# A decoder block on one core: the attention's projections, the fold of V and the output projection as four column tiles of 32

## Chip, cores and metric

The kernel runs on one NeuronCore of a Trainium2 chip, everything in float32. Times are device microseconds of one execution. For the kernel before, the median of three runs is 2486.4 us (2485.95 to 2489.06).

## What is computed

The reference is a decoder layer with three blocks, each followed by a residual addition and a layer norm. Cut to what matters here:

```python
# x: (4, 1024, 512); 32 heads of 16
q = lin(lin(x, wq_w, wq_b), vq_w, vq_b)     # k and v alike
scores = einsum('cbqh,cbkh->cbqk', q, k) / sqrt(16)
o = einsum('cbqk,cbkh->cbqh', softmax(scores), v)
x = layernorm(x + lin(o, wo_w, wo_b))
x = layernorm(x + gated_convolution(x, ctx))        # two taps, four gates
x = layernorm(x + quantised_feed_forward(x))
```

Only the attention and its projections are touched by the change.

## The kernel before

**Set-up (L297 to L352).** The two linear maps in front of q, k and v are multiplied into one matrix each. For q and k this happens at once (L344, matmuls of the whole array, 512 columns wide). For v it is left to small pieces: `fold_v` (L394) makes 128 rows by 256 columns of the folded matrix `w_v`.

**Units (L357).** The attention works on 32 units: 4 batches by 8 groups of 4 heads. A unit's q and k lie in four quadrants of 32 partitions, one per head (16 rows of the head, a row for the softmax's maximum, and padding). For each unit three things are done on TensorE:

- `nat` (L436): scores with queries on the partitions, whose row maxima VectorE reduces at L465. A head's contraction is 32 rows deep, so each multiplication uses a row tile of the array, 32 rows by 128 columns. One call makes two heads, 512 keys each.
- `scores` (L502): scores with keys on the partitions, again in row tiles, 256 queries wide (L519). ScalarE makes the exponentials from them (L530).
- `weigh` (L535): the exponentials times v. The contraction is over 128 keys and the result is 16 values and a sum per head, so four heads stand side by side: each multiplication uses a column tile of 128 rows by 32 columns and writes 32 partitions of the tile `av` (L545). One call is 16 multiplications: 4 blocks of keys, 4 heads in turn.

**Pieces between them.** Work for later units is cut into pieces of four multiplications that accumulate into one PSUM tile over the 512 features (FT = 4 blocks of 128): `project` (L376, q and k of two units, 176 or 160 tokens wide, evicted by ScalarE at L386), `project_v` (L403, 128 tokens by 256 columns of v, added to its bias by VectorE at L411), `fold_v` (evicted by ScalarE at L401), and `out_piece` (L428), which calls `Handed.project` (L217) for 128 tokens by 256 columns of the output projection. Each of the four multiplications has 128 rows of contraction and a result of 128 partitions, so it uses the whole array. The pieces, `scores` and `weigh` take their PSUM tiles in turn from one pool of four banks, `ps_st` (L354); `nat` has a pool of its own.

**Order.** The attention's order is written out by hand: engines get their instructions as the Python loop emits them. Twelve projection pieces and five folds stand in a row at the start (L619). Then, in units 0 to 30 (L674 to L708), a unit has 32 half-steps. Each half-step emits a `nat` for the next unit and a `scores` for this one. After half-step 1, 5, 9, ... comes a `weigh`, after half-step 3, 7, 11, ... one piece:

```python
for work in (nat(u + 1, i, half), scores(u, i, 1 - half)):
    work()
if h % 4 == 1 and weighing:
    weigh(*weighing.pop(0))
...
if h % 4 == 3:
    weighing.append((u, h // 4))
    if fill:
        fill.pop(0)()
    elif u > 24 or u == 24 and h > 24:
        out_pieces.pop(0)()
```

Unit -1 (before the first) and unit 31 (the last) have loops of 16 steps (L642 to L672). In unit -1 each step has one or two pieces after its `nat` calls. In unit 31 every second step has a `weigh` with an output piece directly behind it.

**After the attention** comes the `tail` (L726): the second half of the output projections (L763, through the same `Handed.project`, 512 columns wide), the gated convolution and the feed-forward block.

How the profile counts: a float32 multiplication of the program is two weight loads (LDWEIGHTS) and two MATMULs in the trace, so a piece has 8 MATMULs and a `weigh` 32.

Of the kernel before, what the change touches and what calls it, by code (L numbers as in the profile page):

```python
# [14 lines left out]
P = 128  # L15
# [3 lines left out]
FT = D // P  # L19
# [9 lines left out]
@with_exitstack  # L29
def decoder_kernel(ctx: ExitStack, tc: tile.TileContext, a, out):  # L30
    nc = tc.nc

    outer = ctx.enter_context(tc.tile_pool(name="outer", bufs=1))
    ident = outer.tile([P, P], F32, tag="ident", name="ident")
    make_identity(nc, ident)
    eps = outer.tile([P, 1], F32, tag="eps", name="eps")
    nc.gpsimd.memset(eps, EPS)

    dram = ctx.enter_context(tc.tile_pool(name="dram", bufs=1, space=bass.MemoryType.DRAM))
    attn_d = [dram.tile([D, S], F32, tag=f"attn{b}", name=f"attn{b}") for b in range(B)]


    shared = ctx.enter_context(tc.tile_pool(name="shared", bufs=1))
    hand = Handed(tc, a, shared, attn_d, eps)
    with ExitStack() as attn:
        attention(attn, tc, a, attn_d, ident, shared, hand)
    with ExitStack() as rest:
        tail(rest, tc, a, out, ident, eps, hand)  # L50


class Handed:
# [160 lines left out]
        nc.vector.tensor_mul(scale, tmp, ok)  # L214
        self.scale, self.inv = scale, inv

    def project(self, b, t, cols, pt, bias=False):  # L217

        nc = self.nc
        attn_t = self.big[b][:, 0 : FT * S].rearrange("p (t s) -> p t s", t=FT)  # L220
        for f in range(FT):
            nc.tensor.matmul(  # L222
                pt, attn_t[:, f, t * P : (t + 1) * P], self.w_o[:, f, cols], start=f == 0, stop=f == FT - 1
            )
        y = self.y[b]
        if bias:
            nc.vector.tensor_add(y[:, t, cols], y[:, t, cols], self.b_o[:, cols])
        nc.vector.tensor_add(y[:, t, cols], pt, y[:, t, cols])
        if cols.stop == D:
            nc.vector.bn_stats(self.stats[b][:, t, :], y[:, t, :])  # L230


def attention(ctx, tc, a, attn_d, ident, shared, hand):
    nc = tc.nc
# [4 lines left out]
    w_v = shared.tile([P, FT, D], F32, tag="w_v", name="w_v")  # L239
# [18 lines left out]
    for i in range(2):  # L258
        t = (once if i else shared).tile([P, NT, NH * VW + 15], F32, tag=f"v_sb{i}", name=f"v_sb{i}")
# [9 lines left out]
    for n, pool in ((3, shared), (1, once)):  # L269
        t = pool.tile([P, 8 if n == 3 else 2, S], F32, tag=f"qk{n}", name=f"qk{n}")  # L270
# [9 lines left out]
    for i in range(2):  # L280
        t = once.tile([P, 32], F32, tag=f"neg{i}", name=f"neg{i}")
        nc.gpsimd.memset(t, 0.0)
        negs.append(t)
    for i in range(2):
        t = once.tile([P, S], F32, tag=f"rbc{i}", name=f"rbc{i}")
# [11 lines left out]
    xts = {}  # L297
# [7 lines left out]
    pt = ps.tile([P, P], F32, tag="ps", name="idle_ps")  # L305
    for n in range(10):
        nc.tensor.matmul(pt, idle, idle, start=True, stop=True)
    for which, (w, v, dst) in enumerate((("wq", "vq", b_q), ("wk", "vk", b_k), ("wv", "vv", None))):
        w_n = sp.tile([P, FT, D], F32, tag="w_n", name=f"w_n{which}")
        v_t = sp.tile([P, FT, D], F32, tag="v_t", name=f"v_t{which}")  # L310
# [48 lines left out]
    QW = 256  # L359
# [4 lines left out]
    def to_quadrants(u, which, packed):  # L364

        dst = (q_ts, k_ts)[which][u % 4]
        for j in range(4):
            h = u % 2 * 4 + j
            nc.sync.dma_start(dst[32 * j : 32 * j + HD, :], packed[h * HD : (h + 1) * HD, :])
        if which == 0 and u >= 4:  # L370
            nc.sync.dma_start(dst[HD::32, :], dst[HD + 1 :: 32, :])
# [4 lines left out]
    def project(p, which, t0, n, packed):  # L376

        b, gg = divmod(p, 4)
        w, bias = ((w_q, b_q), (w_k, b_k))[which]
        cols = slice(t0, t0 + n)  # L380
        pt = ps_st.tile([P, QW], F32, tag="st", name=f"proj{p}_{which}_{t0}")
        for f in range(FT):
            nc.tensor.matmul(  # L383
                pt[:, 0:n], w[:, f, gg * P : (gg + 1) * P], xts[b][:, f, cols], start=f == 0, stop=f == FT - 1
            )
        nc.scalar.activation(packed[:, cols], pt[:, 0:n], AF.Identity, bias=bias[:, gg : gg + 1], scale=1.0)  # L386
        if t0 + n == S:
            to_quadrants(2 * p, which, packed)
            if which == 0 and p > 0:
                late_rows.append(lambda: to_quadrants(2 * p + 1, 0, packed))  # L390
            else:
                to_quadrants(2 * p + 1, which, packed)

    def fold_v(f, half):  # L394
        cols = slice(half * QW, half * QW + QW)
        pt = ps_st.tile([P, QW], F32, tag="st", name=f"fold2_{f}_{half}")
        for m in range(FT):
            nc.tensor.matmul(
                pt, w_n[:, m, f * P : (f + 1) * P], v_t[:, m, cols], start=m == 0, stop=m == FT - 1
            )  # L400
        nc.scalar.copy(w_v[:, f, cols], pt)  # L401

    def project_v(b, t, half):  # L403

        pt = ps_st.tile([P, QW], F32, tag="st", name=f"v{b}_{t}_{half}")
        cols = slice(half * QW, half * QW + QW)
        for f in range(FT):
            nc.tensor.matmul(  # L408
                pt, xts[b][:, f, t * P : (t + 1) * P], w_v[:, f, cols], start=f == 0, stop=f == FT - 1
            )  # L410
        nc.vector.tensor_add(  # L411
            v_sb[b % 2][:, t, 16 * half * VW : 16 * (half + 1) * VW].rearrange("p (c h) -> p c h", h=VW)[
                :, :, 0:HD
            ],
            pt.rearrange("p (c h) -> p c h", h=HD),
            b_v[:, cols].rearrange("p (c h) -> p c h", h=HD),
        )

    def qk_pieces(p, which):


        parts = [(0, 176), (176, 176), (352, 176), (528, 176), (704, 160), (864, 160)]
        return [lambda part=part: project(p, which, *part, packs[:, which, :]) for part in parts]

    def v_pieces(b, t):
        return [lambda half=half: project_v(b, t, half) for half in range(2)]

    def out_piece(b, t, half):  # L428
        pt = ps_st.tile([P, QW], F32, tag="st", name=f"po{b}_{t}_{half}")
        hand.project(b, t, slice(half * QW, half * QW + QW), pt)  # L430

# [180 lines left out]

    outs = [(0, t) for t in range(NT)] + [(2, t) for t in range(NT)]
    out_pieces = [lambda b=b, t=t, half=half: out_piece(b, t, half) for b, t in outs for half in range(2)]

    folds = [lambda f=f, half=half: fold_v(f, half) for f in range(FT) for half in range(2)]
    for piece in qk_pieces(0, 0) + qk_pieces(0, 1) + folds[:5]:  # L619
        piece()  # L620
# [3 lines left out]
    for u in range(-1, NU):  # L624
# [48 lines left out]
        else:  # L673
            for h in range(HS):  # L674
                i, half = divmod(h, 2)
# [343 lines left out]
```

## Time and profile before

| | |
|---|---|
| median of 3 runs | 2486.4 us |
| the profiled execution's own time | 2487.75 us |
| its span, first to last instruction | 2486.0 us |
| mean granted TensorE clock | 0.996 |
| TensorE matmuls, weight loads | 25492 each |
| 126 to 1559 us (attention, units 0 to about 24): busy PE, DVE, ACT | 1429.65, 1023.42, 913.29 us |
| 1559 to 1926 us (rest of the attention up to unit 31): busy PE, DVE, ACT | 364.88, 269.43, 225.64 us |
| 1926 to 1976 us (unit 31): busy PE, DVE, ACT | 48.76, 19.01, 35.51 us |
| 1976 to 2486 us (tail): busy PE, DVE, ACT | 485.41, 367.21, 113.31 us |

PE is TensorE's matmuls, PEld its weight loads, DVE is VectorE, ACT ScalarE, POOL GpSimd and SP SyncE. A row of the groups reads: line, engine, operation, what it writes from what it reads, the shape, how many; then the busy time of the group in us, the mean duration of one in ns, and the idle time of the engine in front of them with what ended it. Shapes of matmuls begin with the part of the array that is used, rows by columns: 32\*128 is a row tile, 128\*32 a column tile, 128\*128 the whole. A row of the timeline reads: start in us, length in us, engine, line, operation and how many were merged into it. The end of a matmul is modelled by the profiler, its start is recorded; so distances between starts are what can be relied on, and "single records" below are starts of single instructions in the trace.

### The profile page before, as it was taken

To read this page: it belongs to the slowest core of one execution; us is meant where nothing else is said; L and a number is where in the kernel's file an instruction comes from. 1 tells how busy PE (TensorE), PEld (TensorE's weight loads), DVE (VectorE), ACT (ScalarE), POOL (GpSimd) and SP (SyncE) were. 2 spreads that over 40 slices of the span, in tenths; PEclk is the share of its full clock that TensorE was granted. 3 is DMA by queue.
4 is the path that set the end of the run, shared out by engine and by line. 5 is a ranking of instruction groups with operands and counts; after the bars stand their busy time and mean duration, and the time that the engine had idled before them with its cause. 6 is when DMAs were issued, how large, how long until landed. Compare 5 with 4: busy or idle time off the path is not lost.

```text
span 2486.0 us, 60152 instructions
## 1 busy us (share of the span) xinstructions
PE 2452.5 (99%) x25492; PEld 1781.1 (72%) x25492; DVE 1748.6 (70%) x2198; ACT 1306.5 (53%) x2558; POOL 333.5 (13%) x275
## 2 busy tenths in 40 slices
PE   9999999999999999999999999999999999999998
PEld 6677777777777777777777776677776799547984
DVE  3767777777777777777777777777777465888568
ACT  1166666666666666666666666666655511411132
POOL 2000000000000000000000002000020265311640
PEclk9999999999999999999999999999999999999999
DMA  6101111111110211101111114110120243240311
GB/s 216 48 11 20 20 25 54 21 23 22 23 26 16 58 21 20 21 20 23 22 21 21 24 20 134 21 24 16 25 79 11 66 157 136 84 153 18 119 35 68
DMA packets 80653, 120.80 MB, mean 49 GB/s; under 512 B 39056, under 2 KB 39056, under 8 KB 80384
## 3 DMA queue, kind: packets, MB, share of 16 engines
q1 hardware_dynamic: 79808, 115.90, 16.5%
q8 instruction: 201, 3.29, 0.6%
q10 hardware_dynamic: 576, 1.05, 0.1%
q14 instruction: 68, 0.56, 0.1%
HBM read 80.77 MB, written 18.35 MB: 40 GB/s over the span
## 4 chain that ended last, share of the span: by engine, by line
PE 91%; DVE 5%; POOL 2%; DMA 0%; ACT 0%; issue 0%; SPq 0%; DVEq 0%; POOLq 0%
PE nat L449 22%; PE av L545 19%; PE st L519 18%; PE proj L383 10%; PE v L408 5%; PE po L222 5%; PE pa L792 5%; PE pc L792 5%; PE fold L344 1%; PE pf L878 1%; POOL w L161 1%; DVE y L116 1%; DVE y L883 1%; DVE y L909 1%; DVE xq L864 1%; DVE stats L884 1%
## 5 line engine op out<-in xcount | busy, mean ns | idle before, releaser
L465 DVE TENSOR_REDUCE mx<-nat 128x2 f32<-128x1024 f32 x1008 | 1187.7, 1219 | 453.2 <-PE st L519 424.4
L530 ACT ACTIVATE at<-st 128x512 f32<-128x512 f32 x2016 | 1042.4, 603 | 625.5 <-PE st L519 610.0
L449 PE MATMUL nat<-qk 32*128 32x512 f32 x4032 | 1013.3, 614 | 3.8 <-DVE mx L465 3.8
L519 PE MATMUL st<-qk 32*128 32x256 f32 x8064 | 999.2, 387 | 0.0
L519 PEld LDWEIGHTS st<-qk 32*128 32x128 f32 x8064 | 656.0, 184 | 45.7 <-issue 3.1
L545 PE MATMUL av<-at,v_sb 128*32 128x256 f32 x8192 | 498.8, 382 | 0.6 <-ACT at L530 0.6
L449 PEld LDWEIGHTS nat<-qk 32*128 32x128 f32 x4032 | 343.3, 184 | 174.1 <-DVE mx L465 120.3
L545 PEld LDWEIGHTS av<-at,v_sb 128*32 128x32 f32 x8192 | 241.3, 110 | 223.4 <-ACT at L530 90.5
L592 POOL TENSOR_TENSOR o_n<-o_sb,rbc 128x512 f32<-128x512 f32 x64 | 96.1, 1523 | 1694.3 <-DMA rbc<-rec_d 1233.9
L383 PE MATMUL proj<-xT,w_qk 128*128 128x176 f32 (+1 forms) x1536 | 270.2, 320 | 0.7 <-ACT w_qk L349 0.7
L383 PEld LDWEIGHTS proj<-xT,w_qk 128*128 128x128 f32 x1536 | 223.7, 189 | 64.6 <-ACT at L530 60.0
L792 PE MATMUL pc<-xf,w 128*128 128x171 f32 x1024 | 161.9, 310 | 6.0 <-DVE u L796 4.4
L792 PE MATMUL pa<-xf,w 128*128 128x171 f32 x1024 | 161.4, 310 | 0.0
L792 PEld LDWEIGHTS pc<-xf,w 128*128 128x128 f32 x1024 | 153.6, 191 | 7.7 <-DVE u L796 4.9
L792 PEld LDWEIGHTS pa<-xf,w 128*128 128x128 f32 x1024 | 153.7, 191 | 0.0
L803 ACT ACTIVATE u<-u,b_c 128x512 f32<-128x512 f32 x64 | 45.5, 720 | 170.7 <-DVE u L802 170.7
L408 PE MATMUL v<-w_v,xT 128*128 128x256 f32 x512 | 126.0, 391 | 0.0
L222 PE MATMUL po<-w_o,big 128*128 128x256 f32 (+1 forms) x384 | 118.9, 459 | 2.1 <-ACT at L530 2.1
L878 PE MATMUL pf<-w_f,xq_t 128*128 128x512 f32 x256 | 117.2, 602 | 3.8 <-DVE y L883 2.3
L408 PEld LDWEIGHTS v<-w_v,xT 128*128 128x128 f32 x512 | 92.5, 189 | 34.4 <-ACT at L530 16.6
L222 PEld LDWEIGHTS po<-w_o,big 128*128 128x128 f32 x384 | 70.3, 190 | 49.2 <-issue 31.6
L558 DVE TENSOR_TENSOR o_sb<-av,o_sb 128x256 f32<-128x256 f32 x128 | 54.3, 424 | 72.0 <-PE av L545 71.5
(97 smaller groups left out, 1213.2 us busy)
## 6 DMA issues: line engine op xcount, KB each, us to landing
qk<-qk SPq DMA_DIRECT2D x256, 64.0 KB
w<-in_conv_wT SPq DMA_DIRECT2D x32, 512.0 KB
u<-in_ctx SPq DMA_DIRECT2D x16, 1024.0 KB
xT<-in_xT SPq DMA_DIRECT2D x16, 512.0 KB
rbc<-rec_d SPq DMA_DIRECT2D x128, 64.0 KB
attn<-o_n SPq DMA_DIRECT2D x256, 32.0 KB
big<-attn SPq DMA_DIRECT2D x4, 2048.0 KB
y<-in_x SPq DMA_DIRECT2D x4, 2048.0 KB
```

The lines of the kernel that those rows point to most:

```text
L222: nc.tensor.matmul(pt, attn_t[:, f, t * P : (t + 1) * P], self.w_o[:, f, cols], start=f == 0, stop=f == FT - 1)
L383: nc.tensor.matmul(pt[:, 0:n], w[:, f, gg * P : (gg + 1) * P], xts[b][:, f, cols], start=f == 0, stop=f == FT - 1)
L408: nc.tensor.matmul(pt, xts[b][:, f, t * P : (t + 1) * P], w_v[:, f, cols], start=f == 0, stop=f == FT - 1)
L449: nc.tensor.matmul(pts[n], q_ts[u % 4][r : r + 32, qt * P : (qt + 1) * P], k_ts[u % 4][r : r + 32, kh * 512 : kh * 512 + 512], start=True, ...
L465: nc.vector.tensor_reduce(mxs[u][:, qt, 2 * pair : 2 * pair + 2, kh], pt, AX.X, ALU.max, negate=True)
L519: nc.tensor.matmul(st[:, k * QW : k * QW + QW], k_ts[u % 4][r : r + 32, kt * P : (kt + 1) * P], q_ts[u % 4][r : r + 32, qq * QW : qq * QW ...
L530: nc.scalar.activation(at, st, AF.Exp, scale=0.25)
L545: nc.tensor.matmul(av[32 * j : 32 * j + 32, :], v_sb[b % 2][:, kt, c * VW : c * VW + 32], ats[u, 2 * i + n // 2, j][:, n % 2 * QW : n % 2 ...
L558: nc.vector.tensor_add(o, av, o)
L592: nc.gpsimd.tensor_mul(o_n[:, :, half * 256 : half * 256 + 256], o_sb[:, cols].rearrange("p (s e) -> p e s", e=2), rbc[:, cols].rearrange( ...
L792: nc.tensor.matmul(pt, w[:, i, tap, o : o + P], xf[:, tap, i, :], start=i == 0, stop=i == FT - 1)
L878: nc.tensor.matmul(pt, xq_ts[b, t][:, f, :], hand.w_f[:, f, :], start=f == 0, stop=f == FT - 1)
```

## The change

A new helper, `by_quarters`, does the four multiplications of a piece as sixteen: for each block of the contraction, four multiplications with 32 columns of the stationary matrix each, that write 32 partitions each of the same PSUM tile. `project`, `fold_v`, `project_v` and `out_piece` use it; the tail's `Handed.project` of 512 columns and the folds of L344 stay as they were. The sums, their order over the features, the moving operands and the evictions are the same.

```diff
+def by_quarters(nc, pt, lhsT, rhs):
+    for f in range(FT):
+        for j in range(4):
+            r = slice(32 * j, 32 * j + 32)
+            nc.tensor.matmul(pt[r, :], lhsT(f)[:, r], rhs(f), start=f == 0, stop=f == FT - 1)
...
-    def project(self, b, t, cols, pt, bias=False):
+    def project(self, b, t, cols, pt, bias=False, quarters=False):
...
-        for f in range(FT):
-            nc.tensor.matmul(
-                pt, attn_t[:, f, t * P : (t + 1) * P], self.w_o[:, f, cols], start=f == 0, stop=f == FT - 1
-            )
+        if quarters:
+            by_quarters(nc, pt, lambda f: attn_t[:, f, t * P : (t + 1) * P], lambda f: self.w_o[:, f, cols])
+        else:
+            for f in range(FT):
+                nc.tensor.matmul(
+                    pt, attn_t[:, f, t * P : (t + 1) * P], self.w_o[:, f, cols], start=f == 0, stop=f == FT - 1
+                )
...
-        for f in range(FT):
-            nc.tensor.matmul(
-                pt[:, 0:n], w[:, f, gg * P : (gg + 1) * P], xts[b][:, f, cols], start=f == 0, stop=f == FT - 1
-            )
+        by_quarters(nc, pt[:, 0:n], lambda f: w[:, f, gg * P : (gg + 1) * P], lambda f: xts[b][:, f, cols])
...
-        for m in range(FT):
-            nc.tensor.matmul(
-                pt, w_n[:, m, f * P : (f + 1) * P], v_t[:, m, cols], start=m == 0, stop=m == FT - 1
-            )
+        by_quarters(nc, pt, lambda m: w_n[:, m, f * P : (f + 1) * P], lambda m: v_t[:, m, cols])
...
-        for f in range(FT):
-            nc.tensor.matmul(
-                pt, xts[b][:, f, t * P : (t + 1) * P], w_v[:, f, cols], start=f == 0, stop=f == FT - 1
-            )
+        by_quarters(nc, pt, lambda f: xts[b][:, f, t * P : (t + 1) * P], lambda f: w_v[:, f, cols])
...
-        hand.project(b, t, slice(half * QW, half * QW + QW), pt)
+        hand.project(b, t, slice(half * QW, half * QW + QW), pt, quarters=True)
```

## The prediction

> **What bounds the kernel now.** I read four views in this order: the page (who is busy, what the chain that ended last is made of), the groups by shape (what one instruction of each kind takes), TensorE's timeline round one piece of each kind, and the durations line by line. The page first:
>
> ```profile
> PE 2452.5 (99%) x25492; PEld 1781.1 (72%) x25492; DVE 1748.6 (70%) x2198; ACT 1306.5 (53%) x2558; POOL 333.5 (13%) x275
> ...
> PE 91%; DVE 5%; POOL 2%; DMA 0%; ACT 0%; issue 0%; SPq 0%; DVEq 0%; POOLq 0%
> PE nat L449 22%; PE av L545 19%; PE st L519 18%; PE proj L383 10%; PE v L408 5%; PE po L222 5%; PE pa L792 5%; PE pc L792 5%; PE fold L344 1%; PE pf L878 1%; POOL w L161 1%; DVE y L116 1%; DVE y L883 1%; DVE y L909 1%; DVE xq L864 1%; DVE stats L884 1%
> ```
>
> TensorE sets the end: 91% of the chain is its own work. Inside the attention it never waits long for anybody; in the list of its waits the score maxima (nat for the reduction of L465) hold it 3.8 us in all. So time taken from TensorE's path in the attention comes off the total, as long as nobody else becomes late. "99% busy" can't tell where such time lies, since an overlapped matmul is counted to its modelled end. The groups give the shapes:
>
> ```profile
> L449 PE MATMUL nat<-qk 32*128 32x512 f32 x4032 | 1013.3, 614 | 3.8 <-DVE mx L465 3.8
> L545 PE MATMUL av<-at,v_sb 128*32 128x256 f32 x8192 | 498.8, 382 | 0.6 <-ACT at L530 0.6
> L383 PE MATMUL proj<-xT,w_qk 128*128 128x176 f32 x1024 | 185.0, 325 | 0.7 <-ACT w_qk L349 0.7
> L408 PE MATMUL v<-w_v,xT 128*128 128x256 f32 x512 | 126.0, 391 | 0.0
> ```
>
> Every f32 multiplication is two MATMULs with two weight loads (x512 for 256 calls of L408). nat and st use row tiles (32*128), av already uses column tiles (128*32), and proj, v, po the whole array (128*128). av's 8192 have 498.8 us, 61 ns each; v's 512 have 126.0, 246 ns each. Four column tiles thus take what one whole-array matmul of the same 256 columns takes. The timeline round one v piece and one av:
>
> ```profile
> 396.67 0.38 PE L519 MATMUL st<-qk 32*128 32x256 f32 x2
> 396.99 1.99 PE L408 MATMUL v<-w_v,xT 128*128 128x256 f32 x8
> 398.92 0.70 PE L449 MATMUL nat<-qk 32*128 32x512 f32 x2
> ...
> 400.53 0.38 PE L519 MATMUL st<-qk 32*128 32x256 f32 x2
> 400.85 1.93 PE L545 MATMUL av<-at,v_sb 128*32 128x256 f32 x32
> 402.72 0.70 PE L449 MATMUL nat<-qk 32*128 32x512 f32 x2
> ```
>
> This is the comparison that decides. From the last score to the next one it is 2.25 us across v and 2.19 across av, and av has exactly the form that v is to get: eight groups, 128 rows of contraction, 256 columns. By the single records the medians are 2.242 (52 v pieces) and 2.182 (249 av).
>
> ```profile
> L408 PEld LDWEIGHTS v<-w_v,xT x512: 186/190/190, 79.0 to 1505.0; 128*128 128x128 f32 x171
> L408 PE MATMUL v<-w_v,xT x512: 379/379/483, 79.0 to 1505.2; 128*128 128x256 f32 x171
> ...
> L545 PEld LDWEIGHTS av<-at,v_sb x8192: 105/110/177, 126.4 to 1973.4; 128*32 128x32 f32 x200
> L545 PE MATMUL av<-at,v_sb x8192: 379/379/634, 126.4 to 1973.6; 128*32 128x256 f32 x200
> ```
>
> And this says why. All MATMULs take 379 but a piece's first, whose weights nothing hides: 483 in v (+104), 403 in av (+24, first rows of the av of 400.85).
>
> [...] 0.316 us from the last score into v, proj and av alike, and 0.308 out of v, 0.309 out of av. So the change keeps both drains; a column tile is as foreign to row tiles as the whole array is. [...] the second load of a piece starts 107 ns after the first in v, 28 after it in av. [...] Here the four of a group start 6.7 ns apart (20 ns in all) and groups follow every 216 ns, as v's single ones do.
>
> **The change, part by part.**
>
> Entry of a piece. Before, first to second MATMUL is 320 ns (107 of loading + 213 of streaming); in av, first to second group is 240. Gain 80 ns. For the narrower proj the streaming is 147 (176 columns) or 134 (160), the load is the same 107, so the gain is the same 80.
>
> Body. The six further steps are 216 ns each in v and av; in proj they are 149 and 136, since a load of 107 is hidden behind them already. Quarters change nothing here: 0.
>
> Exit. The last group's fourth tile starts 20 ns after the first, and the drain counts from it: loss 20 ns. Net 60 ns a piece, which is the 2.242 - 2.182 above.
>
> Count. In units 0 to 30 every fourth half-step has one piece: 31 x 8 = 248; unit -1 has 16 places with one or two (only the first of two pays an entry). 264 x 0.060 = 15.8 us.
>
> Last unit: six po pieces stand directly behind an av. Before, L545 to L222 is a change of mode (0.309); after, both are column tiles and the drain goes. At most that saves 196 ns each. But po starts 65 ns after the exponential that frees its bank, so it can come only some 25 ns earlier; with the load, 0.09 x 6 = 0.5 us.
>
> The start: 12 proj and 5 fold pieces in a row pay one entry: 0.1 us. The new change of mode in front of them lies in the 1.27 us that proj waits for the copies of L349 and L351.
>
> What is added: 2368 MATMULs become 9472, each with a load: 14,208 instructions more, all on TensorE's queue. No DMA is moved, no wait added (a piece waits before its first quarter, as before its first matmul), and ScalarE, VectorE, GpSimd and SP keep their instructions in their order. Their fetching is hidden if TensorE's supply keeps up; that is the first rival.
>
> What is late next? ScalarE, behind the 160-column pieces:
>
> ```profile
> 150.92 2.06 ACT L530 ACTIVATE at<-st 128x512 f32<-128x512 f32 x4 [1.73 <-PE st L519]
> 152.99 0.39 ACT L386 ACTIVATE qk<-proj,b_k 128x160 f32<-128x160 f32 x1
> ```
>
> The four exponentials end at 152.98, 12 ns before the eviction starts. With the piece 60 ns shorter the eviction waits for them, some 48 ns. The bank it frees is needed by the weights of a score 0.55 us after the scores resume, and that matmul streams 0.75 after; with 0.107 for the load there are 90 ns of room. It fits, and no more than that. After v, VectorE is free 0.44 us before it is wanted.
>
> Sum: 15.8 + 0.5 + 0.1 = 16.4 us. The profiled execution took 2487.75 (span 2486.0, 1.75 around it), so 2471.3 there; the median of the runs is 1.35 lower, 2486.4 - 16.4 = 2470.0. Bounds of the one size that I took from av alone: if the 20 ns at the exit don't show and the drain in the last unit goes whole, 264 x 0.080 + 1.3 = 22.4 us, 2464; if half of ScalarE's 48 ns came through on the 180 proj pieces, 4.3 us less gain, 2474.
>
> **The rivals.**
>
> *TensorE's instruction supply becomes the bound (slower).* A cycle of four half-steps with an av and a proj piece has 88 loads with their matmuls in 7.12 us (81 ns each), after it 112. From 7.12 / 112 = 63.6 ns a pair on, the change loses. [...] At 66 ns: (112 x 66 - 7120) = 0.27 us on 248 cycles, 67 us, and at the start, where 12 proj pieces stand together, 32 x 66 = 2.1 us each in place of 1.1 to 1.2, 11 us: 2565. Against it: av keeps 54 ns a pair over 32 pairs; and at 289.903 and 290.028 us TensorE's queue passes two waits that have 12 instructions between them in the program, so these took under 10.4 ns each, where the quarters ask for 17.0 (136 / 8) to 18.6. For it: no stretch of the trace holds such a pace for long. Chance 6%.
>
> *Four tiles reading one moving operand get in each other's way (slower).* av's four read four different at tiles; nothing in the trace reads one in four tiles. From nothing to full serialisation (three more 149 ns streams per step, 3.6 us a piece, over 900 us). I take nothing: the streams are there either way. Chance 3%, at 2600 or more.
>
> *The gain is absorbed (no change).* Scores after a piece resume on ScalarE's or VectorE's release, not on TensorE's drain[...]. The constant 0.316 and 0.308 in all 250 places, also in unit -1, which has no exponentials, speak against the first. 2482. Chance 6%.
>
> **How the numbers follow.** The forecast has 85%, at 2470.0, its own range 2463 to 2476. The other cases lie above, so the range goes up to the absorbed one: 2462 to 2482. A measurement of this kernel can tell some 0.2% (5 us) from no change. Faster by more: 0.85; within: 0.06; slower: 0.06 + 0.03 = 0.09.
>
> **What would show it.** Right: first MATMULs of proj, v and po at about +24 in place of +104 ns; starts of four within 20 ns; last score to next score down by 0.06 (v 2.18, proj 1.71 to 1.65 and 1.60 to 1.54); nat and st unchanged. Wrong: groups of proj further apart than 149 or 136 ns (supply, or the shared operand), most of all between 34 and 48 us, where they stand alone; or TensorE's weight loads of st waiting for L386 with scores resuming late.

## The result and the profile after

The changed kernel takes 2473.68 us (median of 4 runs, 2471.43 to 2475.17), the kernel before 2486.98 (4 runs, 2485.95 to 2489.06): a ratio of 0.9945 with an interval of 0.9927 to 0.9962. The forecast was 2470.0. The profiled executions have spans of 2472.9 and 2486.0 us at granted clocks of 0.995 and 0.996. So 13.1 us were gained by the spans where 16.4 were forecast.

In the changed kernel every quartered matmul has line L59, that of the helper; nat is L452, st L522, av L548, the reduction of the score maxima L468. Its page, with the counts, the queue of the instruction fetches and the chain:

```profile
PE 2438.2 (99%) x32596; PEld 1695.6 (69%) x32596; DVE 1749.3 (71%) x2198; ACT 1305.5 (53%) x2558; POOL 333.5 (13%) x275
...
q8 instruction: 256, 4.19, 0.7%
...
PE 91%; DVE 5%; POOL 1%; DMA 1%; issue 0%; ACT 0%; SPq 0%; DVEq 0%; POOLq 0%
```

TensorE still makes 91% of the chain, with 7104 more matmuls and as many more loads, and the other engines have the same instructions. Queue 8, which fetches instructions, has 256 packets of 16 KB instead of 201. The timeline round one v piece and one av:

```profile
393.90 1.93 PE L59 MATMUL v<-w_v,xT 128*32 128x256 f32 x32
395.76 0.70 PE L452 MATMUL nat<-qk 32*128 32x512 f32 x2
...
397.37 0.38 PE L522 MATMUL st<-qk 32*128 32x256 f32 x2
397.70 1.93 PE L548 MATMUL av<-at,v_sb 128*32 128x256 f32 x32
```

Now v and av are alike: 1.86 us from their first matmul to the next score where v had 1.93. By the single records, last score to next score is 2.182 us for v (2.242 before), 1.648 and 1.542 for the two widths of proj (1.708 and 1.602), 2.182 for po, and 2.182 for av as before. The pauses at the change of form are as before too: 0.317 us (0.318) from the last score to a piece's first matmul, and 0.309 from v's last to the next score. Such a pause is called a drain below. The durations line by line show where the 80 ns at the entry went:

```profile
L59 PE MATMUL proj<-xT,w_qk x6144: 298/312/338, 34.0 to 1771.4; 128*32 128x176 f32 x133, 128*32 128x160 f32 x66
L59 PE MATMUL v<-w_v,xT x2048: 378/379/404, 78.6 to 1492.9; 128*32 128x256 f32 x187
L59 PE MATMUL po<-w_o,big x1024: 378/379/404, 1547.9 to 1945.7; 128*32 128x256 f32 x171
```

The third number is the longest. A piece's first matmul in v takes 404 ns in place of 483: a load of 32 columns is in front of it, not one of 128.

Where the 13.1 us arose and where some went again can be read by following the same matmul through both traces (how much earlier than before it starts):

| stretch | change of the lead, us | forecast |
|---|---|---|
| start, up to the first nat (0.22 of it in the folds that the change leaves alone) | +0.28 | +0.1 |
| unit -1, 16 stops for pieces | +0.54 | +0.96 |
| units 0 to 30, 248 stops | +14.88 | +14.88 |
| one stretch in unit 24 | -1.5 | 0 |
| one row of scores in unit 29 | -0.27 | 0 |
| unit 31, po behind av | +1.2 | +0.5 |
| tail | -2.0 | 0 |
| sum | +13.1 | +16.4 |

The first and the last stretch also differ between profiles in which they hold the same instructions. In the run with po alone (below) the start is that of the kernel before, and it reaches the first nat 1.06 us earlier; the tail varies by some 2 us. So the rows of the attention are the firm ones.

### The profile page after: what moved, and what is told of

It is laid out like the page before. It is cut to its first block, busy times and chain, and to the rows that moved or that the text cites. A ratio compares the mean times of both kernels' runs of the same rounds, so it can differ in the third digit from the quotient of the medians.

```text
span 2472.9 us, 74360 instructions
## 1 busy us (share of the span) xinstructions
PE 2438.2 (99%) x32596; PEld 1695.6 (69%) x32596; DVE 1749.3 (71%) x2198; ACT 1305.5 (53%) x2558; POOL 333.5 (13%) x275
## 4 chain that ended last, share of the span: by engine, by line
PE 91%; DVE 5%; POOL 1%; DMA 1%; issue 0%; ACT 0%; SPq 0%; DVEq 0%; POOLq 0%
PE nat L452 22%; PE av L548 19%; PE st L522 18%; PE proj L59 10%; PE v L59 5%; PE pa L795 5%; PE pc L795 5%; PE po L59 2%; PE po L234 2%; PE fold L356 1%; PE pf L881 1%; POOL w L170 1%; DVE y L125 1%; DVE y L886 1%; DVE y L912 1%; DVE xq L867 1%
## 5 line engine op out<-in xcount | busy, mean ns | idle before, releaser
L468 DVE TENSOR_REDUCE mx<-nat 128x2 f32<-128x1024 f32 x1008 | 1187.8, 1219 | 439.8 <-PE st L522 412.1
L452 PE MATMUL nat<-qk 32*128 32x512 f32 x4032 | 1014.0, 615 | 4.3 <-DVE mx L468 4.3
L522 PE MATMUL st<-qk 32*128 32x256 f32 x8064 | 1000.0, 388 | 0.0
L522 PEld LDWEIGHTS st<-qk 32*128 32x128 f32 x8064 | 663.2, 184 | 46.6 <-issue 3.7
L548 PE MATMUL av<-at,v_sb 128*32 128x256 f32 x8192 | 499.4, 383 | 0.6 <-ACT at L533 0.6
L452 PEld LDWEIGHTS nat<-qk 32*128 32x128 f32 x4032 | 343.7, 184 | 192.1 <-DVE mx L468 123.8
L548 PEld LDWEIGHTS av<-at,v_sb 128*32 128x32 f32 x8192 | 241.6, 110 | 223.3 <-ACT at L533 91.1
L59 PE MATMUL proj<-xT,w_qk 128*32 128x176 f32 (+1 forms) x6144 | 259.4, 311 | 0.7 <-ACT w_qk L361 0.7
L59 PEld LDWEIGHTS proj<-xT,w_qk 128*32 128x32 f32 x6144 | 181.3, 109 | 82.0 <-ACT at L533 60.0
L59 PE MATMUL v<-w_v,xT 128*32 128x256 f32 x2048 | 122.5, 382 | 0.0
L170 POOL TENSOR_TENSOR w<-w 128x512 f32<-128x512 f32 x64 | 81.0, 1299 | 159.7 <-DMA w<-in_conv_wT 123.1
L59 PEld LDWEIGHTS v<-w_v,xT 128*32 128x32 f32 x2048 | 60.6, 109 | 58.1 <-ACT at L533 16.6
L559 ACT COPY o_sb<-av 128x256 f32<-128x256 f32 x128 | 48.0, 375 | 78.0 <-PE av L548 59.4
```

The costliest lines, as they stand in the source:

```text
L59: nc.tensor.matmul(pt[r, :], lhsT(f)[:, r], rhs(f), start=f == 0, stop=f == FT - 1)
L170: self.nc.gpsimd.tensor_tensor(w[:, i, tap, :], w[:, i, 0, :], w[:, i, 1, :], op)
L452: nc.tensor.matmul(pts[n], q_ts[u % 4][r : r + 32, qt * P : (qt + 1) * P], k_ts[u % 4][r : r + 32, kh * 512 : kh * 512 + 512], start=True, ...
L468: nc.vector.tensor_reduce(mxs[u][:, qt, 2 * pair : 2 * pair + 2, kh], pt, AX.X, ALU.max, negate=True)
L522: nc.tensor.matmul(st[:, k * QW : k * QW + QW], k_ts[u % 4][r : r + 32, kt * P : (kt + 1) * P], q_ts[u % 4][r : r + 32, qq * QW : qq * QW ...
L548: nc.tensor.matmul(av[32 * j : 32 * j + 32, :], v_sb[b % 2][:, kt, c * VW : c * VW + 32], ats[u, 2 * i + n // 2, j][:, n % 2 * QW : n % 2 ...
```

## Experiments

**The same kernel again.**

> The changed kernel as it is, beside the next two on the same chip. Theory (each piece loses 80 ns of weight loading in front of its first matmul and pays 20 ns at its end): the score-to-score time is 2.18 us for v, 1.65 and 1.54 for proj in this profile too, and the attention ends some 15 us earlier than before; the total is 2471 to 2476. What the tail gave back in the first profile (2.0 us at the transposes in front of the feed-forward) and what unit 24 lost (1.5 us) [...] if they belong to the change they come back alike.

Measured: 2472.43 us (5 runs), the kernel before 2487.36 beside it (9 runs): ratio 0.9939, interval 0.9926 to 0.9951. The stops are 2.182, 1.648 and 1.542 us once more, and the tail hands back 2.4 us. So the gain repeats, and so do its losses in this kernel. That they belong to the change doesn't follow: below there are runs that stall in unit 24 as well and lose nothing against the kernel before, and runs that lose nothing in the same tail.

**Two tiles of 64 columns.** If the exposed weight load is the cause, more columns leave more of it: v's first matmul is 104 ns longer than the others with 128 columns (before) and 25 with 32 (after).

```diff
-        for j in range(4):
-            r = slice(32 * j, 32 * j + 32)
+        for j in range(2):
+            r = slice(64 * j, 64 * j + 64)
```

> The same pieces in two column tiles of 64 instead of four of 32. Theory (weight load in front of the first matmul): a load of 64 columns leaves 53 ns instead of 107, the second tile starts 7 ns later, so a piece gains 107 - 53 - 7 = 47 ns instead of 60. Over 264 places 3.4 us of the gain go, and with the six output pieces behind an av (another mode again, so the drain returns, 0.15 us each) 0.9 more: about 4 us above the kernel with four tiles, near 2478. First matmul of a v piece about 430 ns long against 403 and 483. Rival (the gain comes from column tiles as such, or from the mode shared with av): 2474, stops of 2.18 us as with four.

Measured: 2476.38 us (5 runs), ratio 0.996 (0.9946 to 0.9973). The same v piece in its timeline:

```profile
394.14 1.95 PE L59 MATMUL v<-w_v,xT 128*64 128x256 f32 x16
396.02 0.70 PE L452 MATMUL nat<-qk 32*128 32x512 f32 x2
```

1.88 us to the next score, between the 1.93 of the whole array and the 1.86 of quarters. By the single records the stops are 2.195, 1.662 and 1.555 us: 47 ns shorter than with the whole array, where quarters give 60. (The total lies 3.95 us above the quarters of the same chip, where about 4 were expected. That is the weaker evidence: this profile has one stretch of half clock less in unit 24 and one more at 1865 us.) v's longest matmul, the first of a piece, takes 431 ns, between 483 and 404. So the load exposed at the entry follows the columns loaded. One more thing: in unit 31 the drain between av and po stays (309 ns) here, where po has 128 rows by 64 columns and av 128 by 32. With quarters, both have one form, and it is gone: po's first matmul starts 68 ns behind one of av's.

**The preparation in unit 24 taken apart.** In unit 24 the kernel prepares the feed-forward block: GpSimd converts the matrix w_f (L213) and VectorE makes some scalars (L217 to L223). Both kernels stall there. The changed one, VectorE and then GpSimd:

```profile
1534.65 3.31 DVE L222 TENSOR_TENSOR sc<-sc 128x1 f32<-128x1 f32 x1
1537.88 0.14 DVE L223 TENSOR_TENSOR sc<-sc 128x1 f32<-128x1 f32 x1
1537.95 2.34 DVE L468 TENSOR_REDUCE mx<-nat 128x2 f32<-128x1024 f32 x2
```

```profile
1534.31 5.37 POOL L213 TENSOR_SCALAR w_f<-w_f 128x2048 f32<-128x2048 int32 x1
```

A product of one column takes 3.31 us beside GpSimd's conversion (0.16 in the run below, where no conversion stands beside it), and the next one (L223) 0.14. What holds the first isn't shown: L223 multiplies two columns as well, and went through 1.7 us before the conversion's end in the profile, whose spans on GpSimd are rough. The score maxima stand in VectorE's queue behind it, and TensorE waits for them. In the waits of before and of after, this is the row of nat:

```profile
PE nat L449 <- DVE mx L465: 3.8, 2, 3.3
```

```profile
PE nat L452 <- DVE mx L468: 4.3, 2, 3.8
```

The longest one (last column) is 3.3 us before and 3.8 after. What follows it is in the stretches round it, before first (columns: stretch, PE, PEld, DVE, ACT and POOL busy, granted clock, DMA):

```profile
1550.00:1552.00 2.00, 0.53 (x6) 0.50 (x10) 2.00 (x4) 0.00 (x0) 1.93 (x1) 1.00 0.37 66
1552.00:1554.00 2.00, 2.00 (x20) 1.38 (x15) 1.77 (x2) 1.08 (x2) 0.00 (x0) 0.65 0.61 100
1554.00:1556.00 2.00, 2.00 (x22) 0.69 (x20) 1.23 (x1) 1.09 (x2) 0.00 (x0) 0.50 0.67 109
1556.00:1558.00 2.00, 2.00 (x36) 1.25 (x32) 0.42 (x1) 0.00 (x0) 0.00 (x0) 0.99 0.16 31
```

```profile
1538.00:1540.00 2.00, 0.78 (x6) 0.70 (x10) 2.00 (x3) 0.00 (x0) 1.68 (x1) 0.63 0.47 80
1540.00:1542.00 2.00, 2.00 (x22) 1.65 (x16) 0.95 (x2) 0.59 (x2) 0.00 (x0) 0.50 0.62 102
1542.00:1544.00 2.00, 2.00 (x22) 0.87 (x18) 1.50 (x2) 1.30 (x4) 0.00 (x0) 0.50 0.61 100
1544.00:1546.00 2.00, 2.00 (x32) 0.75 (x20) 0.28 (x1) 0.28 (x1) 0.00 (x0) 0.66 0.08 16
```

The clock falls to a half in both: below full in two stretches of before (0.65, 0.50), in four of after (0.63, 0.50, 0.50, 0.66). The clock records of the traces give the times exactly. In the profiles of before and after, the later half clocks begin whole multiples of 3.413 us behind this first one (136, 170, 173 and 272 of them before; 136, 169, 173, 254 and 273 after), and each lasts one or two such steps (but for the last, with which the profile ends). Before has one step here, 1552.61 to 1556.02 us, and after has two:

```profile
1538.52:1541.93 3.41, 2.71 (x18) 2.29 (x22) 2.37 (x3) 0.52 (x2) 1.16 (x1) 0.50 0.57 93
1541.93:1545.35 3.42, 3.42 (x34) 1.52 (x30) 1.86 (x2) 1.66 (x4) 0.00 (x0) 0.50 0.41 70
```

By the single records the pause is 0.43 us longer (3.78 and 3.35), and TensorE then runs at half clock for 2.7 us more (6.1 and 3.4); the other 1.1 of the table's 1.5 us fall there. The experiment leaves the conversion where it is and (`prepare_w_f` does it alone) and moves VectorE's seven operations eight half-steps on:

```diff
                 if h == 21 and u == 24:
+                    hand.prepare_w_f()
+                if h == 29 and u == 24:
                     hand.prepare_rest()
```

> The changed kernel with the preparation of the feed-forward's weights taken apart: GpSimd's conversion stays at half-step 21 of unit 24, VectorE's seven small operations on one column go to half-step 29, when GpSimd has ended. Theory (VectorE's product of two SBUF operands stood 3.3 us behind GpSimd's conversion, TensorE idled 3.8 us for the score maxima, and the clock went to half for some 5 us): the idle time and the slow stretch go, 5 us less than the kernel as it is, about 2469. Rival (another of VectorE's queue takes its place, or the pause only moved): no difference, 2474.

Measured: 2465.27 us (4 runs), ratio 0.9911 (0.9897 to 0.9924), 7.2 us under the changed kernel of the same chip, where 5 were expected. The product that took 3.31 us takes 0.16 in this profile, beside no conversion, and of nat's waits for a reduction only one of 0.5 us, long before unit 24, is left. Whether this also accounts for what the change lost there is told by doing the same to the kernel before.

**The kernel before with its preparation apart, and its quartered twin.** The same edit in both.

> The kernel before, with GpSimd's conversion left at half-step 21 of unit 24 and VectorE's seven small operations moved to half-step 29, as in the run before. Theory: what the change lost there, 1.5 us, is only the longer stall and the half clock that follows it. Taken out of both kernels, the stall costs the kernel before 7.2 - 1.5 = 5.7 us: 2481 to 2482 here, where the kernel before takes 2487.0. The difference between this kernel and its quartered twin is then 15.9 us in the attention and its start, less what the tail gives back (0.6 in the run before of the twin): some 15 to 17 us. Rival: the loss belongs to the pieces themselves and shows wherever VectorE and GpSimd are busy: the difference between the twins stays at 13.3 us, so this kernel is at 2479 or less.

> The quartered kernel with the preparation moved apart, as measured before (2465.3), on the same chip as its unquartered twin. Theory: 2465 to 2466.5, that is 15 to 17 us below the twin. Rival: 13.3 us below it.

Measured: 2482.11 us (21 runs; ratio to the kernel before 0.9983, 0.9977 to 0.999) and 2465.26 us (4 runs; 0.9917, 0.9903 to 0.993), with the kernel before at 2487.14. The twins are 16.9 us apart by medians and 15.7 by their profiled spans, not 13.3. The times alone are no strong proof, since the pair of kernels with the stall, measured again on one chip, was 14.9 us apart. The traces are: the stretch of unit 24 costs the kernel before 5.3 us and the changed one 6.8, so the 1.5 us lie in the stall and the half clock behind it. At the stretches where the changed kernel ran at half speed, the twin's row has a full clock:

```profile
1540.00:1542.00 2.00, 2.00 (x36) 0.93 (x32) 1.74 (x2) 1.52 (x4) 0.00 (x0) 1.00 0.60 98
1542.00:1544.00 2.00, 2.00 (x32) 1.57 (x32) 1.25 (x2) 0.75 (x2) 0.00 (x0) 1.00 0.59 98
```

**Only the output pieces in quarters** (project, fold_v and project_v with whole-array matmuls again).

> Only the output projection's pieces as four column tiles, the other pieces as before. Theory: 26 places between scores at 60 ns make 1.6 us; the six behind an av gain some 0.20 us each, since the change of mode and the load both go (the prediction had given them 0.09): 1.2 us; 2.7 us in all, 2484. If the 0.20 of the last unit came from elsewhere (all stages ahead being early), the last unit gains no more here than 6 x 0.06.

Measured: 2482.55 us (one run; the kernel before 2484.08 beside it), span 2480.5. That is 1.5 us less where 2.7 were expected; one run of each can't tell, as runs of the kernel before lie between 2484.0 and 2490.2 in the experiments above. The po pieces between scores stop TensorE for 2.182 us, all other pieces for 2.242, 1.708 and 1.602 as before, so the effect belongs to each piece by itself. From 1808 us to the end of unit 31 its lead grows from 1.8 to 3.6 us: 1.2 from the drains that go, the rest from the po pieces ahead of them.

This run also tells something of unit 24. Its stall is nearly as long as the changed kernel's, but only one step of half clock follows, and against the kernel before nothing is lost there (lead 1.06 us ahead of it, 1.16 behind):

```profile
PE nat L461 <- DVE mx L477: 4.2, 2, 3.7
```

```profile
1550.42:1553.83 3.41, 3.08 (x22) 2.60 (x24) 2.36 (x3) 0.89 (x2) 0.79 (x1) 0.50 0.59 96
1553.83:1557.20 3.37, 3.37 (x54) 2.05 (x52) 1.91 (x3) 1.28 (x3) 0.00 (x0) 1.00 0.38 63
```

With 64 columns, too, one step follows a stall of 3.3 us, and nothing is lost; with the gates in quarters two steps follow one of 3.5. So most of the 1.5 us is the second step, and the length of the stall doesn't decide whether it comes. What does isn't shown.

**The tail's gates in quarters too.** 1024 program multiplications become 4096, in a part in which TensorE makes nothing but such multiplications. This asks TensorE's supply for the pace of a piece over 150 us, not over 2.

```diff
-            for i in range(FT):
-                nc.tensor.matmul(pt, w[:, i, tap, o : o + P], xf[:, tap, i, :], start=i == 0, stop=i == FT - 1)
+            by_quarters(nc, pt, lambda i: w[:, i, tap, o : o + P], lambda i: xf[:, tap, i, :])
```

> The changed kernel with the convolution's gates in four column tiles too: 1024 of the program's multiplications that follow one another without a change of mode. Theory: their weight loads are hidden already, so there is nothing to gain; 2.33 us per pair of taps as before, a gate and the total unchanged within 2 us (2472 to 2478), give or take the few changes of mode at the transposes. Rival 1 (column tiles are quicker in themselves): the gates gain. Rival 2 (TensorE's instruction supply has a limit near 17 ns each that only long stretches show): the gates, 145 ns for eight instructions over 150 us, get slower.

Measured: 2484.77 us (one run), span 2483.0, 10 us over the changed kernel. The expectation of an unchanged time missed. The steady pace holds, though: groups of four follow every 145 ns in 961 of some 1008 steps, as single matmuls did, that is 18 ns for each load or matmul over stretches of 150 us. What is lost is lost in pauses. TensorE's waits in the tail, of this kernel:

```profile
PE tr L872 <- DVE xq L866: 11.2, 5, 6.2
PE pc L59 <- DVE u L798: 6.0, 4, 2.3
PE pc L59 <- DVE xf L191: 2.4, 1, 2.4
...
PE pa L59 <- issue: 1.4, 3, 0.9
```

and of the changed kernel:

```profile
PE tr L873 <- DVE xq L867: 9.7, 4, 4.8
PE pc L795 <- DVE u L799: 4.4, 2, 2.5
...
PE pc L795 <- DVE xf L191: 1.0, 1, 1.0
```

"issue" has three waits for which the profile shows no release. All three fall where one of GpSimd's sums of taps, which pa multiplies by, waits for a late part of the weights; so a short stop of TensorE's supply isn't shown by them, nor is it excluded. The others are waits for VectorE, which itself was late. In all their rows the two lists differ by 5.7 us of the 10; the rest is not accounted for. What VectorE was late for leads to the tail's loss, below.

**Tile by tile instead of block by block.** The same sixteen multiplications, all four of one tile first.

```diff
-    for f in range(FT):
-        for j in range(4):
+    for j in range(4):
+        for f in range(FT):
```

> The same sixteen multiplications of a piece in the other order: all four blocks of the contraction for the first column tile, then for the second, and so on. Theory: [...] the third tile starts a step late and the fourth about four steps late: a piece takes about 12 steps instead of 8, 0.6 to 0.9 us more at 264 places, 2640 to 2700. Rival (each tile has a queue of its own of any depth): the order is of no consequence, 2474. Rival (one tile after the other): 32 steps, 3500 and more.

Measured: 3068.1 us (one run), span 3066.3; expected were 2640 to 2700. The direction is right and the size is far off:

```profile
400.19 0.38 PE L522 MATMUL st<-qk 32*128 32x256 f32 x2
400.51 4.59 PE L59 MATMUL v<-w_v,xT 128*32 128x256 f32 x32
405.04 0.70 PE L452 MATMUL nat<-qk 32*128 32x512 f32 x2
```

A v piece takes 4.53 us to the next score instead of 1.86. Its single records show the second tile's first matmul 0.893 us after the first tile's, when four of the first tile's eight matmuls have started. So it ran ahead of the other four, which stand before it in the program. The expected 12 steps were an estimate of the author's that rested on nothing measured. From then on the starts come in twos: this piece never had more than two tiles at work. From a piece's first to its last matmul it takes 4.215 us, 19.5 steps of 216 ns, where the quarters block by block need 7: 32 matmuls in about 20 steps are 1.6 at a time. In this kernel, then, it is the order of issue that lets four tiles run at once.

**Pieces directly behind av.** One stop for two, which now share a form:

```diff
-                if h % 4 == 1 and weighing:
-                    weigh(*weighing.pop(0))
+                if h % 4 == 1:
+                    if weighing:
+                        weigh(*weighing.pop(0))
+                    if fill:
+                        fill.pop(0)()
...
                 if h % 4 == 3:
                     weighing.append((u, h // 4))
-                    if fill:
-                        fill.pop(0)()
```

> The pieces directly behind the av, in its mode, instead of two half-steps later: one stop of row tiles in a cycle instead of two. Theory: a drain and a restart go (about 0.65 us per cycle), but the four half-steps in a row make score maxima faster than VectorE takes them (1.22 us each for 0.87) and only two of them fit in PSUM: the third waits some 0.5 us, the fourth 0.4: about 0.84 us. Net 0.2 to 0.3 us worse on 248 cycles, 2515 to 2545. Rival (the drains are what is left to gain and nobody else is late): 0.65 x 248 = 160 us better, about 2313.

Measured: 2639.31 us (one run), span 2637.5. The rival (2313) is out, the theory's direction is right, and its size (2515 to 2545) is short by half. The stop itself does what the rival counted on:

```profile
393.57 1.93 PE L548 MATMUL av<-at,v_sb 128*32 128x256 f32 x32
395.33 1.38 PE L59 MATMUL proj<-xT,w_qk 128*32 128x176 f32 x32
396.63 0.70 PE L452 MATMUL nat<-qk 32*128 32x512 f32 x2
```

proj follows av without a drain, and av and proj stop the scores for 3.36 us in place of 2.18 + 1.65 = 3.83. But the waits turn:

```profile
PE nat L452 <- DVE mx L468: 113.6, 246, 1.5
```

246 times a matmul of nat now waits for a reduction; its weight loads wait for them 294.8 us in all, where the changed kernel has 123.8. The reductions take 1.22 us each and have two PSUM buffers between them and TensorE (`ps_nat`), so a stop of 3.36 us outlasts the 2.44 us of work that the buffers hold. The mean cycle grows from 7.17 to 7.88 us: 0.47 gained, 1.18 lost. Short stops, evenly spread, keep VectorE fed; it is the limit just behind TensorE.

## Why the prediction held, and where its sum was off

*Entry, body and exit.* 80 ns gained, nothing changed, 20 ns lost: right to the nanosecond in all kinds of pieces (60 each). The run with 64 columns confirms the weight load as the cause, and the one with po alone that each piece gains by itself.

*Count.* All 264 stops became 60 ns shorter, but 7 of the 16 in unit -1 gave it back at once: there the row of scores behind the piece grew by 60 ns (590 to 650, say). Its second nats waits for VectorE's reduction, whose end didn't move; in the single records the matmul starts 56 ns after it in both kernels. That is the "absorbed" rival at work in a corner, -0.4 us. The prediction held up against it the constant 0.316 and 0.308 us at a piece's edges; but these edges say nothing of a wait later in the row. Nor are they constant "in all 250 places, also in unit -1": out of proj it is 0.243 or 0.229 us, and into a piece of unit -1, behind a nat of 512 columns, 0.517.

*Last unit.* The mechanism was right, the size not: not 0.09 but the whole 0.197 us per piece, 1.2 us in all. The step that failed: "po starts 65 ns after the exponential that frees its bank, so it can come only some 25 ns earlier". In the changed kernel po begins while av's last three streams are still to come:

```profile
1918.03 2.06 PE L548 MATMUL av<-at,v_sb 128*32 128x256 f32 x29
1919.79 0.38 PE L59 MATMUL po<-w_o,big 128*32 128x256 f32 x1
1919.92 0.39 PE L548 MATMUL av<-at,v_sb 128*32 128x256 f32 x3
1920.00 2.04 PE L59 MATMUL po<-w_o,big 128*32 128x256 f32 x31
```

The exponential in question ends at 1920.17, after po's first matmul. The 65 ns were a coincidence, not a release. The bound from above that the prediction kept (196 ns) was the truth.

*ScalarE's 90 ns of room behind the 160-column pieces.* It held: these stops shrank by 60 ns like the others, and nat and st are as they were.

*The supply rival* (63.6 ns for a pair) is refuted: the twelve projections at the start, 768 loads and matmuls in a row, take 13.80 us in place of 13.86, 18 ns for each instruction, 36 for a pair. Its 66 ns for a pair were an assumption of the author's that no trace shows. *Four tiles reading one operand* get in nobody's way: the groups keep their 216, 149 and 136 ns.

*What the sum didn't have* is that somebody else does become late, at three places; 3.8 us went there. In unit 24 it was the stall, which cost 1.5 us more, mostly by a second step at half clock. The prediction had its 3.8 us of waits before it and said that TensorE "never waits long for anybody"; 3.3 of them are one stop. In unit 29 it was 0.27 us: a score waits for VectorE's eviction of a po, which stands behind the negation of the maxima (L471, L474 after); that took 1.23 us in place of 1.02, where its median is 0.19. The tail, which the change doesn't touch, gave back 2.0 us at one wait: tr for xq, 2.6 us at the longest before and 4.8 after. That wait ends a chain that starts with the transfer of the convolution's weights and goes on through GpSimd's sums of taps. The last such transfer's issues on SP, before and after:

```profile
2102.95 2.31 SPq L155 DMA_DIRECT2D w<-in_conv_wT  x4
```

```profile
2088.71 3.15 SPq L164 DMA_DIRECT2D w<-in_conv_wT  x4
```

And the sums on GpSimd that wait for it:

```profile
2109.41 3.78 POOL L161 TENSOR_TENSOR w<-w 128x512 f32<-128x512 f32 x3 [6.75 <-DMA w<-in_conv_wT]
```

```profile
2096.59 3.75 POOL L170 TENSOR_TENSOR w<-w 128x512 f32<-128x512 f32 x3 [8.16 <-DMA w<-in_conv_wT]
```

6.75 us of waiting became 8.16; the two transfers ahead of it lost 0.9 and 1.3 us likewise. In the single records the first of the four issues took 1.34 us in place of 0.51, and a fetch packet of queue 8 was in flight just then. This is no single case: of SP's 1290 issues, 37 take more than 0.85 us in the kernel before and 33 of them have a fetch packet in flight; after, 64 and 63. Of the shorter issues, 1 in 12 and 1 in 9 have one. The added instructions bring 55 more packets, and 27 more issues are slow. With the gates in quarters there are 304 packets, and seven of GpSimd's sums wait over 0.4 us for a late part of the weights, where after has two and before none. That fits with the growing loss in the tail. It isn't shown that the packets are the cause: no run changed them alone, and the quartered kernel with its preparation apart has the same 256 packets and loses 0.5 us against the kernel before, or nothing in its repeat. Tile by tile, also with 256 packets, only 40 issues are slow. And the tail moves as much without the change: in the profile of the kernel before with its preparation apart, again with 201 packets, it is 2.3 us shorter than in that of the kernel before, and in the run with po alone 1.9. So whether the 2.0 us are the change's at all stays open.

The forecast missed by 3.7 us and stayed inside its range because the range was wide enough for terms that it didn't have. The part that it was about, 60 ns at each stop, needed no luck.

## What to carry to other kernels

Where pieces of whole-array work stand between tiled ones, as here, the first weight load behind a drain showed, and its price followed its columns (483, 431 and 404 ns for the first matmul with 128, 64 and 32): cut the stationary operand into column tiles, issued block by block in turn, and only the first tile's load shows. A saving of 60 ns counts where TensorE alone ends the row behind it; look in each stage for the release that comes next, not only at the edges of the piece. And before a forecast is closed, look for stalls that both kernels have: one of 3.3 us cost 5.3 with the half clock behind it, and moving seven small operations of VectorE brought 7.2 us on top of the change's 14.9 on the same chip (best version: 2465.3 us).

## What the runs showed of the hardware that was not expected

- With tile-by-tile order the second tile's first matmul starts 0.893 us after the first tile's, about four steps of 216 ns, when four of the first tile's eight matmuls have started.
- Between multiplications of one form, 128 rows by 32 columns, there was no drain even when they belong to different operations: in the changed kernel po's first matmul starts at 1919.79 us, before av's last three (1919.92). Between 128 by 32 and 128 by 64 it is there (309 ns, in the run with 64 columns).
- The half clock comes in steps of 3.413 us, behind pauses of different lengths. In unit 24 TensorE was idle for 2.3 of the 3.41 us ahead of it in the kernel before (1549.20 to 1552.61) and for 3.1 in the changed one (1535.11 to 1538.52). In the tail of the changed kernel it follows a pause of 2.5 us, the longest wait of pc for u:

```profile
2001.70:2003.70 2.00, 1.94 (x10) 1.94 (x11) 1.86 (x5) 0.06 (x1) 0.00 (x0) 0.76 0.88 307
2003.70:2005.70 2.00, 2.00 (x9) 2.00 (x8) 1.86 (x4) 0.66 (x1) 1.09 (x1) 0.50 1.05 408
```

- Both kernels have a pause of 2.12 us in front of a po (1875.21 to 1877.34 us before, 1861.72 to 1863.84 after), and the clock stays full behind it. Of two pauses of nearly one length in front of tr, that of before (2.32 us, to 2417.34) has no half clock behind it, that of after (2.31 us, to 2404.29) has one from 2405.51.
- Nearly all of SP's slow issues (63 of 64 over 0.85 us in the changed kernel; their median is 1.35 us, that of the others 0.55) had an instruction-fetch packet in flight. But so had 140 of the short ones, so a packet alone doesn't make an issue slow.
